# Weighing two steps' exponentials together in the last attention group, with seven tiles of exponentials in turn

## The chip, the cores and the metric

The kernel runs on one core of a Trainium2 chip. The metric is the device time of one execution in microseconds (us); the lower, the better. PE is TensorE, PEld its loading of weights, DVE is VectorE, ACT is ScalarE, POOL is GpSimd and SP is SyncE.

## The reference

One transformer layer over 4096 tokens of 256 features, all in float32: causal attention with 16 heads of 16 features, then a gated feed-forward network with 1024 hidden features, each between layer norms and with a residual.

```python
qkv = layernorm(x) @ w_attn + b_attn            # 16 heads of 16
logits = q @ k^T * 16 ** -0.5, causal
x = x + layernorm(softmax(logits) @ v @ w_proj + b_proj)
h = silu(xn @ w1^T * w1_s) * (xn @ w2^T * w2_s)  # xn = layernorm(x)
h = gelu(h @ h1^T * h1_s);  h = gelu(h @ h2^T * h2_s)
x = x + layernorm(h @ w3^T * w3_s)
```

## The kernel before

The tokens are cut into 8 blocks of 512 (QB), and a block into four tiles of 128 (P). The 16 heads are four groups of four. The attention's work is a list `items` of 32 pairs (j, g), block of queries and group of heads, in the order of j and then g. For an item the loop runs over `kt`, the tiles of 128 keys up to the diagonal: 4 (j + 1) steps, 32 in the last block. One step makes the scores of 128 keys by 512 queries for four heads, their exponentials, and the product of these with the values.

- **Scores** (`ScoreUnit`). A unit is one pair `pr` of the group's two pairs of heads. `products` (L664) issues four matmuls: keys by queries for either head, and a second product that subtracts each query's maximum (`mrow`, `ones`). They lie in half the array's rows each, in tiles of 64*128, and two run side by side. A unit's result fills two PSUM banks: either one tile of two banks of the pool `ps_s` (two such tiles), or, if the unit is `alone`, two single banks of the pool `ps_m` (three banks). Where no maxima are taken in the step, every third unit is alone.
- **Exponentials** (`finish`, L679). ACT writes them to a tile `e` of 128 by 2 by 512, from the pool `ep` with five buffers: one instruction of 1024 elements for a unit in `ps_s`, two of 512 for a unit alone. In the four steps on the diagonal, POOL then zeroes what lies above it (L684).
- **Weighing** (`Values.step`, L714). Four heads' exponentials are the moving operand, the values the stationary one, in tiles of 128*32, into one PSUM bank `av` of the pool `ps_av`, which has one buffer. Over an item's steps the products add up in this bank. The trace has eight matmul records for a step's weighing, two passes of four. After an item's last step ACT copies the bank to `av_sb` (L723) and SP stores it (L725). `Values` is a queue: `add` puts a step's tiles in with the time from which they may be weighed, `LAG` = 2 after it, and `step` weighs the foremost if it is due. `now` advances by two a step. So the weighing of step kt - 1 stands behind the scores of step kt.
- **Maxima** (`MaxUnit`, L581, L594, L598). The maxima of an item to come are found beside the scores of an item before it: products of TensorE into `ps_m`, reduced by DVE. `due` pairs of such units go with each step. When the last item begins, all maxima are done, `pairs` is empty, and its steps hold scores, exponentials and weighings alone.
- **Background work** (`bg`) goes on between the steps: norms and projections of other blocks. In block 7 it is finished before the last group.

Every engine executes its instructions in the order in which the program issues them (`manual_schedule`); the waits between engines and for free buffers follow from the tiles. The tags "o" and "T" of the pool `wk1` (one buffer each, 128 by 2 by 512) serve the projection (`Room.features`) and the features of a block that is prepared (`xT`).

After the last item the queue of `Values` is emptied, and `feed_forward` begins with products `za` (L1007).

Of the kernel before, what the change touches and what calls it, by code (L numbers as in the profile page):

```python
# [10 lines left out]
F32 = mybir.dt.float32  # L11
# [6 lines left out]
P = 128  # L18
QB = 512
# [48 lines left out]
def sandwich_kernel(  # L68
# [119 lines left out]
    def weight_pieces(key, tags):  # L188

        return {  # L190
            (c, o): piece(tag, f"{key}_{c}_{o}", F32R) for (c, o), tag in tags.items()
        }
# [7 lines left out]
    def load_pieces(src, tiles):  # L200
        for (c, o), t in tiles.items():
            nc.sync.dma_start(
                out=t.bitcast(F32), in_=src[c * P : (c + 1) * P, o * QB : (o + 1) * QB]
            )
# [133 lines left out]
    with ExitStack() as actx:  # L338
# [3 lines left out]
        wk1 = actx.enter_context(tc.tile_pool(name="wk1", bufs=1))  # L342
        qp = actx.enter_context(tc.tile_pool(name="qp", bufs=3))
        ep = actx.enter_context(tc.tile_pool(name="ep", bufs=5))
# [4 lines left out]
        def bank(name):  # L349
            return ps_m.tile([P, 512], F32, tag="m", name=name)  # L350
# [114 lines left out]
        def queries(j, g):  # L465

            qT[j, g] = [
                load_rows(f"q{pr}", f"q{pr}_{j}_{g}", "q", j, 4 * g + 2 * pr) for pr in range(2)
            ]
# [14 lines left out]
        def ask(n, kt):  # L484

            while asked[0] < len(chunks) and chunks[asked[0]][0] <= n + 2:

                if asked[0] >= RING and chunks[asked[0] - RING] >= (n, (kt - 1) // NT):
                    return
                if n >= 2 * G and kt % 2:  # L490
                    return
                keys(*chunks[asked[0]])
                if n >= 2 * G:
                    return
# [74 lines left out]
        class MaxUnit:  # L569
            def __init__(self, j, g, t, c, pr, n, mx, neg, mcol):  # L570
                self.at = j, g, t, c, pr
                self.n, self.mx, self.neg, self.mcol = n, mx, neg, mcol
                self.ps = {h: bank(f"pm_{j}_{g}_{t}_{c}_{h}") for h in (2 * pr, 2 * pr + 1)}
                self.diagonal = c == j
# [14 lines left out]
            def finish(self):  # L589
                j, g, t, c, pr = self.at  # L590
                n = self.n
                for h, ps in self.ps.items():
                    if not self.diagonal:
                        nc.vector.tensor_reduce(  # L594
                            self.mx[:, h, c : c + 1], ps[:, 0:n], AX.X, ALU.max
                        )
                        continue
                    nc.vector.tensor_tensor_reduce(  # L598
                        out=ps[:, 0:n],
                        in0=ps[:, 0:n],  # L600
                        in1=mask[:, QB - n : QB],
                        scale=1.0,
                        scalar=-3.0e38,
                        op0=ALU.add,
                        op1=ALU.max,
                        accum_out=self.mx[:, h, c : c + 1],
                    )
                if not (self.diagonal and pr == 0):
                    return False
                neg, mcol = self.neg, self.mcol  # L610
                nc.vector.tensor_reduce(
                    neg[:, t, :], self.mx[:, :, 0 : j + 1], AX.X, ALU.max, negate=True
                )
                if t < NT - 1:
                    return False
                high = stat.tile([P, NT, 4], F32R, tag="high", name=f"high_{j}_{g}")
                nc.vector.tensor_copy(high, neg)

                col = mcol.rearrange("p t (i pr e) -> p t pr i e", i=2, pr=2)
                by_pair = [a.rearrange("p t (pr i) -> p t pr i", pr=2) for a in (neg, high)]  # L620
                nc.vector.tensor_copy(col[:, :, :, :, 0], by_pair[1])
                nc.vector.tensor_tensor(col[:, :, :, :, 1], *by_pair, ALU.subtract)
                return True

            def to_rows(self):
# [12 lines left out]
                nc.vector.tensor_copy(mrow, ps)  # L638
                mT[j, g] = mrow

        class ScoreUnit:


            def __init__(self, j, g, kt, pr, alone=False):
                self.at = j, g, kt, pr
                c, tt = divmod(kt, NT)
                self.k = kT[G * j + g, c, pr][:, tt * P : (tt + 1) * P]
                self.diagonal = c == j
                self.q0 = tt * P if self.diagonal else 0
                name = f"s_{j}_{g}_{kt}_{pr}"  # L650

                if alone:
                    self.ps = [bank(f"{name}_{i}") for i in range(2)]
                else:
                    both = ps_s.tile([P, 2, QB], F32, tag="s", name=name)
                    self.ps = [both[:, i, :] for i in range(2)]
                self.sources = [p[:, None, :] for p in self.ps] if alone else [both]
# [14 lines left out]
            def finish(self):  # L672
                j, g, kt, pr = self.at
                q0 = self.q0
                e = ep.tile([P, 2, QB], F32, tag="e", name=f"e_{j}_{g}_{kt}_{pr}")
                at = 0
                for ps in self.sources:
                    n = ps.shape[1]
                    nc.scalar.activation(e[:, at : at + n, q0:], ps[:, :, q0:], AF.Exp)  # L679
                    at += n  # L680
                if self.diagonal:

                    at = e[:, :, q0 : q0 + P]
                    nc.gpsimd.affine_select(  # L684
                        out=at,
                        in_=at,
                        compare_op=ALU.is_ge,
                        fill=0.0,
                        base=0,
                        pattern=[[0, 2], [1, P]],  # L690
                        channel_multiplier=-1,
                    )
                return e
# [101 lines left out]
        items = [(j, g) for j in range(NB) for g in range(G)]  # L795
# [28 lines left out]
        values = Values()  # L824
# [27 lines left out]
        for n, (j, g) in enumerate(items):  # L852
            if n + 2 < len(items):
                queries(*items[n + 2])
            if g == G - 1 and j + 2 < NB:
                bg.finish(("prep", j + 2))

            if (j, g) == (NB - 2, 0):
                for key in ("w1", "w2"):
                    W[key] = weight_pieces(key, TAGS[key])  # L860
                    load_pieces(rounded[key], W[key])
            if (j, g) == (NB - 1, G - 2):
                for _ in halving:
                    pass
                bg.add(("norm", 0), norm_block(0, room, first_features), NORM)
            if (j, g) == (NB - 1, G - 1):
                W["h1"] = weight_pieces("h1", TAGS["h1"])
                load_pieces(rounded["h1"], W["h1"])
            item = j, g
            if g == G - 1:  # L870
                issued += len(ahead)
                ahead.clear()
            begun = issued
            goal = min(first[min(n + 2, len(items))] + LEAD, first[-1])
            for kt in range(count[n]):
                ask(n, kt)
                if (g, kt) == (0, 2) and j + 2 < NB:
                    bg.add(("prep", j + 2), prep(j + 2), PREP)
                due = begun + (goal - begun) * (kt + 1) // count[n] - issued
                pairs = [next(stream) for _ in range(due)]  # L880
                issued += due
                es = []
                if pairs:
                    issue(MaxUnit(*pairs[0][0]))
                es = [
                    issue(ScoreUnit(j, g, kt, pr, not pairs and next(alone)))
                    for pr in range(2)
                ]
                if pairs:
                    issue(MaxUnit(*pairs[0][1]))  # L890
                values.step(now + 1)
                for pair in pairs[1:]:
                    for args in pair:
                        issue(MaxUnit(*args))
                now += 2
                values.add(j, g, kt, max(kt - NT * j, 0) * P, es, now - 1)
                rows_of(now)
                bg.pace(count[n] - kt + count[n] * max(G - 2 - g, 0))
                if j > 0 and kt % 4 == 2 and kt < NT * j:
                    next(halving, None)  # L900
            rows_of(now + 2)
            if n == len(items) - 2:
                count_low()
# [230 lines left out]
```

## Time and profile before

| | us |
|---|---|
| median of three runs | 2488.5 (2483.43 to 2493.22) |
| the profiled execution, its own time | 2495.86 |
| its span in the profile | 2494.2 |
| busy: PE / DVE / ACT / POOL | 2395.7 / 1786.7 / 1309.1 / 561.6 |
| the last group, from its first score to the feed-forward's first product | 1728.49 to 1798.00 |

The profile is of one execution. Its page gives the busy time of each engine, the chain of work that ended last, and groups of instructions by line. The other views are answers about stretches of the same trace: instructions in order of time (start, length, engine, line, what is written from what; a wait stands in brackets with what ended it), and the busy time of each engine in a stretch, with the share of full speed that TensorE's clock was granted (PEclk). Records that follow each other on an engine and are of one kind are merged in the timeline ("x4"); a merged row has the start of its first record.

### The profile page before, as it was taken

Reading aid. Unit: us, or ns where it says so; the run is one execution under the profiler, and the core shown is the slowest. Engines: PE = TensorE matmul, PEld = TensorE weight load, DVE = VectorE, ACT = ScalarE, POOL = GpSimd, SP = SyncE. Lnnn points to the kernel's source line nnn. Section 1 sums busy time; section 2 is a strip of 40 time slices with the busy share of each in tenths; the row PEclk is TensorE's granted clock in tenths of the full one; section 3 lists DMA queues with packets and bytes.
Section 4 is the critical chain, followed back from the end, with each engine's and each line's share of the span. In section 5 each row is a group of like instructions: output and inputs, shape, how many; then the busy total and the mean of one; then the engine's idle time right before and its main releaser. Section 6 shows DMA issues by size and latency. Waiting matters only on the chain.

```text
span 2494.2 us, 40139 instructions
## 1 busy us (share of the span) xinstructions
PE 2395.7 (96%) x15237; PEld 1434.2 (58%) x15237; DVE 1786.7 (72%) x3838; ACT 1309.1 (52%) x1710; POOL 561.6 (23%) x898
## 2 busy tenths in 40 slices
PE   4899999999999999999999999999999999999998
PEld 2545545545554555455555555544488787887887
DVE  1667988888897989799999888986145535554553
ACT  1336666665675667666667667766822222222221
POOL 2325333423343233322422222000001200000000
PEclk8779999999999999999999999999999999999999
DMA  4444434323333322424222231111111100000000
GB/s 145 150 141 141 151 115 152 120 82 130 107 126 117 116 72 96 151 94 133 84 74 72 88 109 60 51 56 56 47 54 35 34 1 18 17 17 1 17 9 10
DMA packets 134825, 202.73 MB, mean 81 GB/s; under 512 B 14912, under 2 KB 59584, under 8 KB 134624
## 3 DMA queue, kind: packets, MB, share of 16 engines
q1 hardware_dynamic: 132672, 198.75, 24.3%
q8 instruction: 122, 2.00, 0.3%
q10 hardware_dynamic: 1776, 1.18, 0.2%
q14 instruction: 79, 0.65, 0.1%
q0 software_dynamic: 176, 0.15, 0.1%
HBM read 137.91 MB, written 62.13 MB: 80 GB/s over the span
## 4 chain that ended last, share of the span: by engine, by line
PE 82%; DVE 11%; issue 2%; DMA 2%; ACT 1%; POOL 1%; SPq 0%; ACTq 0%; POOLq 0%; DVEq 0%
PE av L714 20%; PE s L664 18%; PE z L1007 18%; PE pm L581 16%; DVE mx L594 3%; DVE pm L598 2%; PE pyf L1076 2%; DVE fa L1048 2%; PE pk L426 1%; PE py L249 1%; PE pv L543 1%; PE pq L426 1%; PE pmt L630 1%; PE za L1007 1%; PE zb L1007 1%
## 5 line engine op out<-in xcount | busy, mean ns | idle before, releaser
L679 ACT ACTIVATE e<-s 128x1024 f32<-128x1024 f32 (+3 forms) x1175 | 1039.1, 936 | 471.1 <-PE s L664 462.3
L594 DVE TENSOR_REDUCE mx<-pm 128x1 f32<-128x512 f32 x1792 | 1111.5, 682 | 153.0 <-PE pm L581 135.4
L581 PE MATMUL pm<-k,q 64*128 64x512 f32 (+3 forms) x2304 | 626.9, 456 | 33.0 <-DVE mx L594 18.6
L581 PEld LDWEIGHTS pm<-k,q 64*128 64x128 f32 x2304 | 325.1, 188 | 533.3 <-DVE mx L594 368.9
L714 PE MATMUL av<-e,v 128*32 128x512 f32 (+3 forms) x4608 | 582.5, 577 | 0.2 <-POOL e L684 0.2
L664 PE MATMUL s<-q,k 64*128 64x512 f32 (+3 forms) x2304 | 472.7, 391 | 4.4 <-ACT xT L533 1.2
L664 PE MATMUL s<-mrow,ones 64*128 64x512 f32 (+3 forms) x2304 | 458.9, 381 | 0.0
L598 DVE CUSTOM_DVE_ANT_0 pm<-pm,mask 128x384 f32<-128x384 f32 (+3 forms) x512 | 240.2, 517 | 78.6 <-PE pm L581 75.7
L1063 ACT ACTIVATE fb<-z,sh 128x512 f32<-128x512 f32 x128 | 88.1, 688 | 388.4 <-PE z L1007 367.2
L664 PEld LDWEIGHTS s<-q,k 64*128 64x128 f32 x2304 | 236.5, 189 | 71.7 <-issue 18.8
L664 PEld LDWEIGHTS s<-mrow,ones 64*128 64x128 f32 x2304 | 241.3, 189 | 38.3 <-DVE mrow L638 0.7
L684 POOL TENSOR_SCALAR_AFFINE_SELECT e<-e 128x256 f32<-128x256 f32 x256 | 102.3, 407 | 620.1 <-ACT e L679 618.0
L1007 PE MATMUL z<-hb_0h,h 128*128 128x512 f32 x512 | 200.8, 392 | 0.0
L1007 PE MATMUL z<-hb_0l,h 128*128 128x512 f32 x512 | 200.0, 391 | 0.0
L714 PEld LDWEIGHTS av<-e,v 128*32 128x32 f32 x4608 | 91.7, 108 | 143.6 <-issue 130.5
L173 POOL TENSOR_TENSOR rstd<-ve,neghalf 128x4 f32<-128x4 f32 (+1 forms) x22 | 20.7, 943 | 662.9 <-DVE ve L171 637.4
L977 DVE CAST hb_1h<-fb 128x512 fp32r<-128x512 f32 x64 | 27.8, 435 | 144.5 <-ACT fb L1063 144.5
L977 DVE CAST hb_0h<-fb 128x512 fp32r<-128x512 f32 x64 | 27.3, 427 | 138.7 <-ACT fb L1063 138.7
L1007 PEld LDWEIGHTS z<-hb_0h,h 128*128 128x128 f32 x512 | 96.8, 189 | 20.0
L1046 ACT ACTIVATE sl<-za,s 128x512 f32<-128x512 f32 x64 | 44.0, 689 | 122.2 <-PE za L1007 64.2
L1007 PEld LDWEIGHTS z<-hb_0l,h 128*128 128x128 f32 x512 | 96.7, 189 | 19.9
L1048 DVE SCALAR_TENSOR_TENSOR fa<-zb,s,sl 128x512 f32<-128x512 f32 x64 | 47.6, 745 | 72.2 <-ACT sl L1046 72.2
(247 smaller groups left out, 2437.8 us busy)
## 6 DMA issues: line engine op xcount, KB each, us to landing
k<-k SPq DMA_DIRECT2D x288, 256.0 KB
q<-q SPq DMA_DIRECT2D x64, 256.0 KB
x<-in_x_dram SPq DMA_DIRECT2D x16, 512.0 KB
k<-hik SPq DMA_DIRECT2D x32, 256.0 KB
k<-lok SPq DMA_DIRECT2D x32, 256.0 KB
q<-hiq SPq DMA_DIRECT2D x32, 256.0 KB
q<-loq SPq DMA_DIRECT2D x32, 256.0 KB
avd<-av_sb SPq DMA_DIRECT2D x32, 256.0 KB
```

Source lines behind the costliest of these rows:

```text
L426: nc.tensor.matmul(ps, lhsT=wqk[d][:, i * D + c * P : i * D + (c + 1) * P], rhs=xTs[j][:, d, :], start=(d == 0), stop=(d == DC - 1),)
L581: nc.tensor.matmul(ps[:, 0:n], lhsT=qT[j, g][pr][r, t * P : (t + 1) * P], rhs=kT[G * j + g, c, pr][r, 0:n], start=True, stop=True,)
L594: nc.vector.tensor_reduce(self.mx[:, h, c : c + 1], ps[:, 0:n], AX.X, ALU.max)
L598: nc.vector.tensor_tensor_reduce(out=ps[:, 0:n], in0=ps[:, 0:n], in1=mask[:, QB - n : QB], scale=1.0, scalar=-3.0e38, op0=ALU.add, op1=ALU ...
L664: nc.tensor.matmul(self.ps[i][:, self.q0 :], lhsT=(self.k, ones[pr])[m][r, :], rhs=(qT[j, g][pr], mT[j, g])[m][r, self.q0 :], start=(m == ...
L679: nc.scalar.activation(e[:, at : at + n, q0:], ps[:, :, q0:], AF.Exp)
L684: nc.gpsimd.affine_select(out=at, in_=at, compare_op=ALU.is_ge, fill=0.0, base=0, pattern=[[0, 2], [1, P]], channel_multiplier=-1,)
L714: nc.tensor.matmul(self.av[h * HW : (h + 1) * HW, q0:], lhsT=vb[kt // NT][:, kt % NT, o : o + HW], rhs=es[h // 2][:, h % 2, q0:], start=(k ...
L977: nc.vector.tensor_copy(hi, full)
L1007: nc.tensor.matmul(ps, lhsT=w[c], rhs=single(part[:, c, :]), start=(c == 0 and i == 0), stop=(c == kc - 1 and i == parts - 1),)
L1048: nc.vector.scalar_tensor_tensor(h, zb, s2[:, oc : oc + 1], sl, ALU.mult, ALU.mult)
L1063: nc.scalar.activation(h, z, AF.Gelu, scale=sc[:, oc : oc + 1])
```

## The change

In the last item the weighing is not called at even steps, and is called twice at odd ones. So two steps' scores follow each other, and then the weighings of the two foremost steps in the queue. The first odd step weighs the last step of the item before it and step 0. At step 3 steps 1 and 2 are weighed, and so on; the last step's is weighed after the loop, as before. As more exponentials are alive at a time, their tiles in the last item go in turn through seven homes: five times the pool `ep`, then the tags "o" and "T" of `wk1`. All other items take `ep` as before.

```diff
+        homes = cycle(range(7))
+
+        def exponentials(name, last):
+
+            n = next(homes) if last else 0
+            if n < 5:
+                return ep.tile([P, 2, QB], F32, tag="e", name=name)
+            return wk1.tile([P, 2, QB], F32, tag="oT"[n - 5], name=name)
+
         class ScoreUnit:
...
                 self.at = j, g, kt, pr
+                self.last = (j, g) == items[-1]
...
-                e = ep.tile([P, 2, QB], F32, tag="e", name=f"e_{j}_{g}_{kt}_{pr}")
+                e = exponentials(f"e_{j}_{g}_{kt}_{pr}", self.last)
...
-                values.step(now + 1)
+
+                if n < len(items) - 1:
+                    values.step(now + 1)
+                elif kt % 2:
+                    values.step(now + 1)
+                    values.step(now + 1)
```

## The prediction

> **What bounds the kernel now.** I began with the page: which engine carries the chain that ended last, and by which lines. I then cut out the one stretch that the change touches, the attention's last group (block 7, group 3), and read its waits.
>
> ```profile
> PE 82%; DVE 11%; issue 2%; DMA 2%; ACT 1%; POOL 1%; SPq 0%; ACTq 0%; POOLq 0%; DVEq 0%
> PE av L714 20%; PE s L664 18%; PE z L1007 18%; PE pm L581 16%; DVE mx L594 3%; DVE pm L598 2%; PE pyf L1076 2%; DVE fa L1048 2%; PE pk L426 1%; PE py L249 1%; PE pv L543 1%; PE pq L426 1%; PE pmt L630 1%; PE za L1007 1%; PE zb L1007 1%
> ```
>
> TensorE carries the kernel, and the two lines whose order changes (scores L664, weighing L714) are the largest. But the shares are of all 32 groups, and only one changes. The busy time by stretch gives that group its size: the first row is the group from its first score to the feed-forward, the second its 26 full steps (kt 2 to 27).
>
> ```profile
> core 0: us, PE busy (x) PEld busy (x) DVE busy (x) ACT busy (x) POOL busy (x), PEclk, DMA share, GB/s
> 1728.49:1798.00 69.51, 68.65 (x522) 27.83 (x521) 0.42 (x2) 61.90 (x87) 3.75 (x9) 0.97 0.05 19
> 1733.86:1789.13 55.27, 55.27 (x421) 21.61 (x418) 0.00 (x0) 51.41 (x70) 0.00 (x0) 1.00 0.00 1
> ```
>
> Only 69.5 of 2494.2 us can move, and a step takes 55.27 / 26 = 2.126 us. TensorE never stands idle, yet ACT is busy for 93% of that time: two engines are close together. The timeline of one step shows where TensorE loses time.
>
> ```profile
> 1744.49 0.50 PE L664 MATMUL s<-q,k 64*128 64x512 f32 x2
> 1744.83 0.40 PE L664 MATMUL s<-mrow,ones 64*128 64x512 f32 x2
> 1745.07 0.39 PE L664 MATMUL s<-q,k 64*128 64x512 f32 x2
> ...
> 1745.32 6.20 ACT L679 ACTIVATE e<-s 128x512 f32<-128x512 f32 x8 [0.18 <-PE s L664]
> ```
>
> ```profile
> 1748.20 0.61 PE L714 MATMUL av<-e,v 128*32 128x512 f32 x4
> ...
> 1748.74 0.50 PE L664 MATMUL s<-q,k 64*128 64x512 f32 x2
> ...
> 1749.08 0.40 PE L664 MATMUL s<-mrow,ones 64*128 64x512 f32 x2
> ...
> 1749.31 0.40 PE L664 MATMUL s<-q,k 64*128 64x512 f32 x2
> ...
> 1749.54 0.40 PE L664 MATMUL s<-mrow,ones 64*128 64x512 f32 x2
> ...
> 1749.87 0.64 PE L714 MATMUL av<-e,v 128*32 128x512 f32 x4
> ```
>
> Read starts, not durations. Pairs of score products follow each other after 0.23 us. The first pair after a weighing needs 0.34 until the next (+0.10), a weighing starts 0.33 after the last pair (+0.10), and the second half of a weighing (from 1748.20) needs 0.54 until the scores, where its first half (0.99 in all, by the chain below) needs 0.45 (+0.09). So one round trip, scores to weighing and back, costs about 0.29 us.
>
> **What the Trainium skill says.** "TensorEngine Tiling (Array Packing)", Key Properties: changing the tiling mode drains the engine. Scores use 64*128 tiles and weighings 128*32, so each step changes twice; the extra gaps agree. "ScalarE: Activation LUTs", What ACT_TABLE_LOAD costs: an ACTIVATE takes 186 ns + 0.833 ns an element and overlaps its neighbour by about 93 ns. That makes 1039 ns for 1024 elements; the rows by shape in this stretch say 1025 (and 597 for 512). So ACT takes a 1024-wide tile every 0.93 us, 1.9 us a step. "TensorE: Matmul & The Clock Gate", Part 1: TensorE's clock is halved after a too idle window of 3.4 us. The trace agrees, as shown with the entry below.
>
> **The change, part by part.** Each group of two steps is now: four score units (a unit is the products of one pair of heads and fills two PSUM banks), then two weighings.
>
> *Removed:* one round trip in two steps, 0.29 us, at most 16 times: 4.6 us. No instruction is added or removed, and no DMA changes place beside others.
>
> *The exponentials' buffers.* Just before a weighing six tiles are alive, so seven suffice. Tags o and T in wk1 are last read by block 6's projection, done near 1508 us by its rows (L249). Their cost is nothing, whether under five or seven names.
>
> *A new wait.* Units alternate over ps_s (two buffers of two banks) and, every third unit (alone), over two of ps_m's three banks. Hence a unit reuses the banks of the unit three before it. Today the trace shows no wait of TensorE for that. In a burst of four, the fourth unit would start 0.34 + 5 x 0.23 = 1.50 us after the first. But the first unit's exponential starts 0.83 us after its products (1745.32 - 1744.49) and takes 1.03, and TensorE resumes 0.05 after ACT (the copy of av_sb ends at 1797.95, za starts at 1798.00): 1.91 us. So the fourth unit **waits 0.41 us**, and both weighings, and the next burst, are queued behind it. Where first and fourth units are both alone, ps_m's third bank is free and the first half of the exponential (597 ns) releases the next: no wait. With period three against bursts of four, that is one burst in three.
>
> A burst with the wait: 1.91 + 0.23 + 0.33 + weighings 3 x 0.45 + 0.54 = 4.36 us, against 4.25 for two steps today: +0.11. Without it: 0.34 + 6 x 0.23 + 0.33 + 1.89 = 3.94: -0.31. The spacing between two weighings is the one number that the trace lacks: at least 0.43 (two passes of 512 columns at the 0.21 us that a pair of scores streams, estimated from the Clock Gate page's 215.7 ns), at most 0.54; I take 0.45, as between the halves. Of the 13 bursts of full steps (kt 2 to 27), 9 wait and 4 don't: 9 x 0.11 - 4 x 0.31 = **-0.25 us**. Bounds: no wait at all -4.0, every burst waiting with 0.09 lost between weighings +2.6.
>
> *Entry, kt 0 and 1.* The previous group's last weighing and kt 0's are now adjacent, and share the one ps_av buffer.
>
> ```profile
> 1729.82 1.94 ACT L679 ACTIVATE e<-s 128x1024 f32<-128x1024 f32 x2 [6.60 <-PE s L664]
> ...
> 1731.64 0.59 ACT L723 COPY av_sb<-av 128x512 f32<-128x512 f32 x1
> ...
> 1732.87 1.07 PE L714 MATMUL av<-e,v 128*32 128x512 f32 x8
> ```
>
> Today the copy that frees ps_av runs beside kt 1's scores. After, ACT has all of kt 1's exponentials ahead of it: four units from 1729.82 at 0.92 to 0.95 end near 1733.7, the copy near 1734.3, and kt 0's weighing starts at 1734.4 where it now starts at 1732.87: **+1.5 us** (bounds 0.8, if ACT's queue is ordered more kindly, and 2.0). TensorE then idles some 1.4 us of 3.4, 40%. The busy time by window shows what that does to the clock (column before DMA share):
>
> ```profile
> 1992.00:1995.40 3.40, 2.15 (x7) 0.78 (x6) 3.02 (x6) 0.35 (x1) 0.00 (x0) 1.00 0.00 0
> 1995.40:1998.80 3.40, 3.40 (x9) 2.64 (x9) 1.12 (x2) 0.69 (x1) 0.00 (x0) 0.50 0.02 5
> 2162.60:2166.00 3.40, 2.31 (x9) 1.13 (x7) 3.26 (x7) 1.19 (x1) 0.00 (x0) 1.00 0.00 0
> 2166.00:2169.40 3.40, 3.18 (x13) 2.42 (x14) 1.71 (x3) 0.69 (x1) 0.00 (x0) 1.00 0.02 5
> ```
>
> 37% idle halved the next window, 32% did not. So I count one halved window; a score pair takes 0.43 there against 0.23 (1729.09 to 1729.51), a step of estimated 3.4 against 2.13 us, and 3.4 us of it lose **1.3 us** (bounds 0 and 2.6, two windows).
>
> *Tail, kt 28 to 31.* Kt 29's weighing moves behind the last scores and covers the exponentials and POOL's masks, for which TensorE now waits 0.17 and 0.21 us before the last weighing: **-0.3 us** (bounds -0.6 and 0).
>
> *Sum:* -0.25 + 1.5 + 1.3 - 0.3 = **+2.2 us**. The profiled execution took 2495.86 us (span 2494.2 and 1.7 around it), so 2498.1 in its terms; it lies 7.4 us over the median 2488.5, so I forecast **2490.7 us**, within 0.5% (12.4 us, about what a measurement of this kernel can tell from no change).
>
> **Rivals.**
> 1. *The wait for banks doesn't come, the drains go.* For it: ACT needs about 1.9 us a step and the new step would take 1.97. Against it: the latency from scores to free banks, 1.9 us, is longer than three units. It gives -4.0 in the full steps, with entry and tail -1.5 to -4.3: about 2485.5.
> 2. *The clock falls again and again (slower).* The same Clock Gate page tells (A second HAM failure mode) of kernels whose small idle gaps between PSUM buffers keep halving it. Place: the 0.41 us waits, 12% of a window. For it: a window with little idle time can fall too. Against it: today none of the 16 windows of the full steps is halved, and 32% idle did not do it. Each halved window costs 1.3 us; from 8 on, with entry and tail, the kernel is slower by over 12.4 us; all 16 give about 2512.
> 3. *Nothing changes,* because weighings don't pair: a step pops only what is due. At odd kt both entries are due by the queue's own times, so this would need an error in my reading: 2488.5.
>
> **How the numbers follow.** My account 0.60, rival 1 0.27, rival 3 0.03, rival 2 0.10, of which half beyond 0.5%. Faster by over 0.5% would need the stretch to lose 12.4 of 69.5 us, more than all drains: only an unrelated shift of the runs gives it, 0.05. So faster 0.05, same 0.90, slower 0.05. The range takes my account's bounds (-3.8 to +7.2), rival 1, and half the spread of the runs (5 us), not all at once: 2481 to 2498.
>
> **What would show it.** Full steps: bursts of about 4.36, 4.36 and 3.94 us in turn; TensorE waiting about 0.4 us before the fourth unit, released by ACT e L679, in two bursts of three; a second weighing 0.45 after the first. Entry: a wait of TensorE for ACT av_sb L723 above 1 us, and PEclk 0.5 after it. I am wrong if the full steps' 55.27 us fall below 52 or rise above 58, or if anything outside 1728 to 1798 us moves.

## The result and the profile after

The changed kernel takes 2495.72 us (median of 22 runs), the kernel before 2491.93 us beside it: a ratio of 1.0017 with a 95% interval of 1.0010 to 1.0024, or 2.5 to 6.0 us more. A second comparison in another session (e9) gave 1.0013 (1.0005 to 1.0022). The change is slightly slower, within the 0.5% that was forecast as no change. The forecast rise of 2.2 us lies just below the first interval and inside the second (1.2 to 5.5 us). The forecast of 2490.7 us for the time itself was 5.0 us too low; 3.4 of these are that the kernel before took 2491.93 us here, and 2488.5 in the runs that the forecast started from.

The profiled execution took 2498.98 us with a span of 2497.3 us. Its chain has the same lines as before (the attention's moved by ten, so L674 is the scores, L724 the weighing, L689 the exponential, L733 the copy to av_sb; the feed-forward's by fifteen, so L1022 is `za` and `z`), with one that was not among the first: ACT's exponential, at 1%.

```profile
PE 81%; DVE 11%; DMA 2%; issue 2%; ACT 2%; POOL 1%; SPq 0%; ACTq 0%; POOLq 0%; DVEq 0%
PE av L724 20%; PE s L674 18%; PE z L1022 18%; PE pm L581 16%; DVE mx L594 3%; DVE pm L598 2%; PE pyf L1091 2%; DVE fa L1063 2%; PE py L249 1%; PE pk L426 1%; PE pv L543 1%; PE pq L426 1%; ACT e L689 1%; PE pmt L630 1%; PE za L1022 1%
```

The busy time by stretch, for the last group and for its 26 full steps. The columns after the length are the busy us of PE, PEld, DVE, ACT and POOL, PEclk, the DMA share and GB/s:

```profile
1728.22:1799.46 71.24, 66.35 (x522) 30.84 (x521) 0.42 (x2) 60.29 (x87) 3.66 (x9) 0.97 0.05 20
1735.23:1791.02 55.79, 53.58 (x420) 24.07 (x416) 0.00 (x0) 49.87 (x69) 0.00 (x0) 1.00 0.01 4
```

TensorE's busy time in the full steps fell from 55.27 to 53.58 us, yet they take 55.79. Half of the changes of tiling went, and with them the time lost at these, but idle time took its place and 0.5 us more. The view of waits, for TensorE in the last group, says what it is idle for (us in total, times, longest):

```profile
PE s L674 <- ACT e L689: 2.6, 10, 0.3
PE av L724 <- ACT av_sb L733: 1.6, 1, 1.6
```

Neither wait was in the trace before. Nine of the ten waits for ACT e fall in the full steps, one in the tail. The chain shows the bursts. Those with a wait run through ACT, and the one between them (from 1739.73) doesn't:

```profile
1735.30 0.69 PE s L674 x4
...
1736.07 1.03 ACT e L689
...
1737.14 0.73 PE s L674 x4
1737.88 1.85 PE av L724 x16
1739.73 2.14 PE s L674 x16
1741.87 1.85 PE av L724 x16
1743.72 0.68 PE s L674 x4
...
1744.48 1.03 ACT e L689
```

In the timeline one sees both waits with the time that TensorE was idle in brackets:

```profile
1733.60 0.58 ACT L733 COPY av_sb<-av 128x512 f32<-128x512 f32 x1
...
1734.23 1.06 PE L724 MATMUL av<-e,v 128*32 128x512 f32 x8 [1.65 <-ACT av_sb L733]
1735.23 0.50 PE L674 MATMUL s<-q,k 64*128 64x512 f32 x2
...
1737.14 0.50 PE L674 MATMUL s<-q,k 64*128 64x512 f32 x2 [0.24 <-ACT e L689]
1737.48 0.40 PE L674 MATMUL s<-mrow,ones 64*128 64x512 f32 x2
1737.81 1.92 PE L724 MATMUL av<-e,v 128*32 128x512 f32 x16
1739.66 0.50 PE L674 MATMUL s<-q,k 64*128 64x512 f32 x2
...
1743.65 0.50 PE L674 MATMUL s<-q,k 64*128 64x512 f32 x2
```

The fourth unit starts 1.91 us after the first (1737.14 - 1735.23). Without the wait it would start at 1736.73, 0.23 us after the pair at 1736.50, so the loss is 0.41 us. The bracket has only 0.24 us, because the third unit's last pair counts as busy until 1736.90: for a queue of matmuls the loss is read from starts. A burst with the wait takes 4.43 us (1735.23 to 1739.66), one without 3.99 (1739.66 to 1743.65), and two steps before the change took 4.25.

| part of the last group, us | before | after | difference |
|---|---|---|---|
| entry, to the first score of step 2 | 5.37 | 7.01 | +1.64 |
| full steps 2 to 27 | 55.27 | 55.79 | +0.52 |
| tail, to the feed-forward's first product | 8.87 | 8.44 | -0.43 |
| sum | 69.51 | 71.24 | +1.73 |

The span grew by 3.1 us. The rest stands in the feed-forward, which took 697.8 us from its first product to the end, against 696.2: its first cast, `ha_0h` (DVE), started 1.92 us after its input was ready in this execution, and 0.1 in the kernel before. Experiments e4, e7, e8 and e11 are about that.

### The profile page after: what moved, and what is told of

Read it like the earlier page. It is cut to its first block, busy times and chain, and to the rows that moved or that the text cites. A ratio compares the mean times of both kernels' runs of the same rounds, so it can differ in the third digit from the quotient of the medians.

```text
span 2497.3 us, 40138 instructions
## 1 busy us (share of the span) xinstructions
PE 2392.1 (96%) x15237; PEld 1437.6 (58%) x15237; DVE 1786.4 (72%) x3838; ACT 1307.3 (52%) x1710; POOL 561.4 (22%) x898
## 4 chain that ended last, share of the span: by engine, by line
PE 81%; DVE 11%; DMA 2%; issue 2%; ACT 2%; POOL 1%; SPq 0%; ACTq 0%; POOLq 0%; DVEq 0%
PE av L724 20%; PE s L674 18%; PE z L1022 18%; PE pm L581 16%; DVE mx L594 3%; DVE pm L598 2%; PE pyf L1091 2%; DVE fa L1063 2%; PE py L249 1%; PE pk L426 1%; PE pv L543 1%; PE pq L426 1%; ACT e L689 1%; PE pmt L630 1%; PE za L1022 1%
## 5 line engine op out<-in xcount | busy, mean ns | idle before, releaser
L689 ACT ACTIVATE e<-s 128x1024 f32<-128x1024 f32 (+3 forms) x1175 | 1037.4, 937 | 470.1 <-PE s L674 465.1
L724 PE MATMUL av<-e,v 128*32 128x512 f32 (+3 forms) x4608 | 577.3, 575 | 1.6 <-ACT av_sb L733 1.6
L674 PE MATMUL s<-q,k 64*128 64x512 f32 (+3 forms) x2304 | 472.4, 391 | 7.2 <-ACT e L689 3.1
L674 PE MATMUL s<-mrow,ones 64*128 64x512 f32 (+3 forms) x2304 | 459.6, 381 | 0.0
L674 PEld LDWEIGHTS s<-q,k 64*128 64x128 f32 x2304 | 237.1, 189 | 66.3 <-ACT e L689 13.7
L674 PEld LDWEIGHTS s<-mrow,ones 64*128 64x128 f32 x2304 | 241.8, 188 | 38.4 <-DVE mrow L638 0.7
L1022 PE MATMUL z<-hb_0h,h 128*128 128x512 f32 x512 | 200.9, 392 | 0.0
L1022 PE MATMUL z<-hb_0l,h 128*128 128x512 f32 x512 | 200.1, 391 | 0.0
L724 PEld LDWEIGHTS av<-e,v 128*32 128x32 f32 x4608 | 93.7, 109 | 147.6 <-issue 129.4
L1022 PEld LDWEIGHTS z<-hb_0h,h 128*128 128x128 f32 x512 | 96.9, 189 | 20.0
L1022 PEld LDWEIGHTS z<-hb_0l,h 128*128 128x128 f32 x512 | 96.7, 189 | 19.9
```

The source lines that it names most:

```text
L674: nc.tensor.matmul(self.ps[i][:, self.q0 :], lhsT=(self.k, ones[pr])[m][r, :], rhs=(qT[j, g][pr], mT[j, g])[m][r, self.q0 :], start=(m == ...
L724: nc.tensor.matmul(self.av[h * HW : (h + 1) * HW, q0:], lhsT=vb[kt // NT][:, kt % NT, o : o + HW], rhs=es[h // 2][:, h % 2, q0:], start=(k ...
L1022: nc.tensor.matmul(ps, lhsT=w[c], rhs=single(part[:, c, :]), start=(c == 0 and i == 0), stop=(c == kc - 1 and i == parts - 1),)
```

## The experiments

Two were the changed kernel itself (e9, e10) and one the kernel before (e8), for further profiles. Ratios are to the kernel before, with 95% intervals; one profile each gives the stretches.

**e1_entry: step 0 weighed as before.**

```diff
+                elif kt == 0:
+                    values.step(now + 1)
                 elif kt % 2:
```

> The changed kernel, but step 0 of the last item calls the weighing once, as before the change, so that the previous group's last weighing no longer stands beside step 0's and ACT's copy of the av bank has step 1's scores to hide behind; pairs from step 3 on as in the changed kernel. Theory (the entry costs the changed kernel 1.6 us, TensorE waiting for the copy av_sb): no wait of TensorE for av_sb above 0.1 us in the last group, first score to feed-forward 69.6 us instead of 71.2, ratio to before 1.0010. Rival (the rise lies elsewhere, in the full steps or in the feed-forward): first score to feed-forward stays above 71, ratio 1.0017.

```profile
1728.21:1797.92 69.71, 66.46 (x521) 30.69 (x521) 0.42 (x2) 60.29 (x87) 3.67 (x9) 0.97 0.06 22
1733.66:1789.45 55.79, 53.57 (x420) 24.04 (x416) 0.00 (x0) 50.30 (x70) 0.00 (x0) 1.00 0.00 1
```

The last group takes 69.71 us, 1.5 less than in the changed kernel; the full steps are the same to 0.01 us. No wait for av_sb is left before the last group's end. So the 1.5 us are the cost of the two neighbouring weighings at the entry. The ratio is 1.0003 (0.9993 to 1.0012), below the 1.0010 that was expected; its interval is too wide to decide alone.

**e2_banks: single banks for the first and fourth unit of each burst.**

```diff
-                    issue(ScoreUnit(j, g, kt, pr, not pairs and next(alone)))
+                    issue(ScoreUnit(j, g, kt, pr, kt % 2 == pr if n == len(items) - 1 else not pairs and next(alone)))
```

> The changed kernel, but in the last item the units that use two single banks are chosen by their place in the burst of four: always the first and the fourth (in the changed kernel every third unit). Theory (two bursts of three lose 0.45 us because the fourth unit waits for the first one's exponential to free its banks): no such wait in any burst, all 13 bursts of full steps at about 4.0 us, 51.9 us for steps 2 to 27 instead of 55.8, first score to feed-forward 67.2 us, ratio to before 1.0001. Rival (ACT's rate or the weighing's own time holds the burst at 4.3 us): steps 2 to 27 stay above 54.5 us, ratio 1.0015 or more.

The first row below is the last group, the second 12 of its 13 bursts of full steps:

```profile
1720.29:1790.15 69.86, 67.33 (x522) 36.65 (x521) 0.42 (x2) 60.89 (x98) 3.62 (x9) 0.95 0.06 21
1732.46:1781.63 49.17, 49.17 (x389) 26.75 (x385) 0.00 (x0) 46.20 (x72) 0.00 (x0) 1.00 0.00 1
```

TensorE's idle time is gone, and a burst takes 49.17 / 12 = 4.10 us. The edit changes only which units use single banks, so the wait was for the banks. The burst is shorter than the 4.25 us of two steps before, but longer than the 4.0 expected (e3 shows why): thirteen of them make 53.3 us, between the expected 51.9 and the rival's 54.5. The group's 69.86 us hold the entry's wait and, after it, one burst at a halved clock (5.39 us, 1.29 over the others). Ratio 0.9993 (0.9983 to 1.0004): below the changed kernel's 1.0017 (1.0010 to 1.0024), not clear of the kernel before.

**e3_both: both edits.**

> The changed kernel with both edits: step 0 weighs as before, and the first and the fourth unit of each burst use single banks. Theory: the gains of the two add, first score to feed-forward 65.6 us (69.5 before the change), ratio to before 0.9985, or 0.9992 if the feed-forward's first cast again waits 1.9 us for the store of av_sb as in the changed kernel's profile. Rival (the 4.6 us of drains can't be had, since ACT becomes the bound as soon as TensorE stops waiting): above 68 us, ratio 0.9995 or more.

The first row is the last group, the second 11 bursts. Then three rows of the timeline around the start of one burst:

```profile
1722.21:1789.21 67.00, 66.28 (x522) 35.58 (x521) 0.42 (x2) 61.00 (x98) 3.62 (x9) 0.97 0.07 23
1735.55:1780.68 45.13, 45.13 (x356) 24.40 (x352) 0.00 (x0) 42.97 (x68) 0.00 (x0) 1.00 0.01 1
```

```profile
1747.89 0.64 PE L674 MATMUL s<-q,k 64*128 64x512 f32 x2
1748.23 0.53 PE L674 MATMUL s<-mrow,ones 64*128 64x512 f32 x2
...
1748.71 2.00 ACT L689 ACTIVATE e<-s 128x512 f32<-128x512 f32 x3 [0.24 <-PE s L674]
```

The group takes 67.0 us, 2.5 less than before the change and 4.2 less than the changed kernel: the gains of e1 and e2 add. About 0.3 of the 2.5 is luck with the clock, which was halved for a shorter part of the entry (5.09 us to step 2's first score, 5.37 before the change). The gain is 1.4 us short of the expected 65.6, since a burst takes 45.13 / 11 = 4.10 us. The merged pair at 1747.89 is 0.64 us long and not 0.50: the unit's two halves start 0.15 us apart (1747.89 and 1748.04). The second starts 0.05 us after the end (1747.99) of ACT's first exponential of the fourth unit before it, whose bank it takes by the order of the pool. So a small wait for banks is left. ACT is busy for 42.97 of 45.13 us, 95%, and idle only 0.24 us before a burst's first exponential. So the rival was half right: ACT still has idle time, but every burst now runs close behind it. Ratio 0.9998 (0.9987 to 1.0010), which decides between neither.

**e4_tiles: the seven tiles alone, nothing paired.**

```diff
-                if n < len(items) - 1:
-                    values.step(now + 1)
-                elif kt % 2:
-                    values.step(now + 1)
-                    values.step(now + 1)
+                values.step(now + 1)
```

> The kernel before with the seven tiles of exponentials in turn alone: every step weighs as before, nothing is paired. Theory (the tiles' places cost nothing): first score to feed-forward 69.5 us, the feed-forward's first cast waits at most 0.2 us for the store of av_sb, ratio to before 1.0000. Rival (the tiles in o and T change what the feed-forward's first tiles must wait for, which is the 1.8 us that the changed kernel lost after the last group): the first cast waits 1.5 us or more, ratio 1.0007.

The last group took 69.17 us and its full steps 55.27, as before the change; the ratio is 1.0005 (0.9996 to 1.0013). The cast waited 1.43 us, near what the rival had foretold (1.5 or more) and against the theory; but e8 shows 1.55 us in the kernel before itself, and e1 with the same tiles 0.32. So the wait needs no tiles in o and T, and they don't always bring it.

**e5_never: no unit on single banks in the last item.**

```diff
-                    issue(ScoreUnit(j, g, kt, pr, not pairs and next(alone)))
+                    issue(ScoreUnit(j, g, kt, pr, n < len(items) - 1 and not pairs and next(alone)))
```

> The changed kernel, but in its last item no unit uses single banks: all alternate over the two double buffers, so a unit reuses the banks of the unit two before it and the suspected wait comes twice a burst. Theory (the latency from a unit's scores to its free banks, 1.91 us, sets the burst): third unit 1.91 us and fourth 2.83 us after the first, bursts of 5.35 us throughout steps 2 to 27, first score to feed-forward about 85 us, TensorE's clock not halved there (idle 1.2 of 5.35 us, 23%), ratio to before 1.0074. Rival (such idle gaps make the clock halve again and again): PEclk 0.5 in four windows or more of the full steps, first score to feed-forward above 90 us, ratio above 1.009.

TensorE's waits over 11 bursts, the starts of the first, third and fourth unit of one burst, and the busy time of the 11:

```profile
PE s L674 <- ACT e L689: 9.9, 22, 0.7
```

```profile
1748.70 0.50 PE L674 MATMUL s<-q,k 64*128 64x512 f32 x2
...
1750.61 0.50 PE L674 MATMUL s<-q,k 64*128 64x512 f32 x2 [0.71 <-ACT e L689]
...
1751.53 0.50 PE L674 MATMUL s<-q,k 64*128 64x512 f32 x2 [0.18 <-ACT e L689]
```

```profile
1743.35:1802.12 58.77, 48.91 (x356) 18.53 (x352) 0.00 (x0) 42.38 (x44) 0.00 (x0) 1.00 0.00 1
```

The third unit starts 1.91 us and the fourth 2.83 us after the first, as expected. 58.77 / 11 = 5.34 us a burst against 5.35 expected, and the clock stayed at full speed (1.00) with TensorE idle for 17% of the time by the records. The group took 87.1 us, 2 more than expected, of which one halved window after the entry is a part. Ratio 1.0070 (1.0047 to 1.0092). So the latency from a unit's scores to its free banks sets the burst, and these gaps didn't halve the clock.

**e6_five: the changed kernel with five tiles.**

```diff
-            n = next(homes) if last else 0
+            n = 0
```

> The changed kernel with the five tiles of exponentials of before also in the last item, none in o and T. Theory (what is waited for is PSUM and ACT; the fourth unit's exponential would have to wait for the first weighing of its burst, which is done before ACT gets there): bursts of 4.43, 4.43 and 3.99 us as in the changed kernel, first score to feed-forward 71.2 us, ratio to before 1.0017. Rival (seven tiles are needed for six alive): ACT waits for the weighing in each burst, bursts above 4.8 us, ratio above 1.003.

```profile
1723.06:1794.83 71.77, 66.51 (x521) 30.79 (x520) 0.42 (x2) 61.19 (x87) 3.70 (x9) 0.97 0.05 19
1730.07:1785.86 55.79, 53.57 (x422) 24.05 (x418) 0.00 (x0) 50.58 (x69) 0.00 (x0) 1.00 0.01 4
```

The full steps take the same 55.79 us with five tiles as with seven, so five tiles don't lengthen a burst. What differs is the tail, 0.5 us longer, where the last exponential waits for POOL:

```profile
1792.82 0.38 ACT L689 ACTIVATE e<-s 128x256 f32<-128x256 f32 x1 [0.54 <-POOL e L694]
```

Ratio 1.0011 (0.9999 to 1.0024).

**e8_before and e4 beside it: the cast's wait.** The kernel before, unchanged.

> The kernel before, unchanged, for a second profile. Theory (the wait of the feed-forward's first cast for the store of av_sb differs from execution to execution and is no part of the change): a wait other than the 0.1 us of the first profile, anywhere up to 1.9 us. Rival (the change makes it): 0.1 us again. First score to feed-forward 69.2 to 69.5 us under both.

The first row is of the first profile of the kernel before, the second of e8, the third of the changed kernel:

```profile
1802.16 0.43 DVE L977 CAST ha_0h<-fa 128x512 fp32r<-128x512 f32 x1
```

```profile
1798.25 0.43 DVE L977 CAST ha_0h<-fa 128x512 fp32r<-128x512 f32 x1 [1.55 <-SPq L1130]
```

```profile
1805.42 0.43 DVE L992 CAST ha_0h<-fa 128x512 fp32r<-128x512 f32 x1 [1.92 <-DMA h<-r_h]
```

The kernel before has the wait too, in another execution: it doesn't take the change to bring it. The brackets name a queue event in one and a load in the other, the event that ended nearest; e7 and e11 are about the store of av_sb.

**e7_both_store and e11_before_store: another place for the last av_sb.** e7 is e3 with this edit, e11 the kernel before with it:

```diff
-                    av_sb = wk1.tile([P, QB], F32, tag="av_sb", name=f"av_sb_{j}_{g}")
+                    name = f"av_sb_{j}_{g}"
+                    av_sb = (
+                        piece("k15_1", name)
+                        if (j, g) == items[-1]
+                        else wk1.tile([P, QB], F32, tag="av_sb", name=name)
+                    )
```

> The kernel with step 0 weighed as before and single banks for first and fourth unit, and the last item's av_sb in the tile of the last weights of h2 (k15_1) instead of wk1's, so that the feed-forward's first cast has no store to wait for. Theory (the cast ha_0h waits for the landing of the last store of av_sb, by chance 0.1 to 1.9 us): the cast waits under 0.1 us, 696.1 us from the feed-forward's first product to the end, first score to feed-forward 67.0 us, ratio to before 0.9985. Rival (the cast waits for other transfers, or the loads of h2 now come late): the cast waits over 1 us again or the products of h2 wait, 697.5 us or more from the feed-forward's first product to the end.

> The kernel before with the last item's av_sb in the tile of the last weights of h2 alone. Theory (the cast's wait for the store is there in most executions, and goes): the cast waits under 0.1 us, about 696.1 us from the feed-forward's first product to the end, ratio to before 0.9995. Rival (the wait only moves, or the weights of h2 come late): 697.5 us or more to the end, ratio 1.0000 or more.

The cast in e7; in e11 it stands 0.84 us after `fa` in the same way:

```profile
1796.51 0.75 DVE L1070 SCALAR_TENSOR_TENSOR fa<-zb,s,sl 128x512 f32<-128x512 f32 x1 [70.92 <-ACT sl L1068]
1797.35 0.43 DVE L999 CAST ha_0h<-fa 128x512 fp32r<-128x512 f32 x1
```

No wait is left in either. Of the eleven profiles with av_sb in wk1 nine have a wait of 1.4 us or more, one 0.32 and one 0.1, so two without any speak for the store; its landing itself is not in the records. From the feed-forward's first product to the end it is 696.3 us in e7 and 696.8 in e11 (which has one more halved window, near 2160 us), against 697.8 in the changed kernel. But the kernel before had 696.2 us in its first profile and 699.3 in e8 (with one more halved window too), so this stretch alone doesn't measure the edit. Ratios: e7 0.9991 (0.9981 to 1.0001), e11 0.9989 (0.9977 to 1.0001). They have the lowest ratios here, and neither is clear of the kernel before. e7's last group took 68.2 us, although the clock was halved for 6.4 us of its entry, and e11's 70.3. The full steps are where profiles repeat best: 55.27 us in all four with the order of before (the first, e8, e4, e11), 55.8 in the changed kernel's order at full clock (the first, e10, e6, e1), 53.4 in e3 and 53.2 in e7. So the pairing does gain 2 us there once the banks fit; the times of the whole kernel are too scattered to show it.

**e9_after and e10_after: the changed kernel again.**

> The changed kernel, unchanged, for a second profile. The last group's own rise was 1.7 us in the first profile, the ratio says 2.5 to 6.0 us. Theory (TensorE's 1.65 us wait at the entry halves the clock in some executions, for 1.3 us a window, according to how the window falls): the same 1.65 us wait and bursts, and either a window of PEclk 0.5 after it and 72.5 us from the last group's first score to the feed-forward, or none and 71.2; ratio to before 1.0012 to 1.0022. Rival (the rest is outside the last group): 71.2 us and something else longer than in both profiles of the kernel before.

> The changed kernel, unchanged, for a third profile, with the same expectations as for the second: 71.2 us from the last group's first score to the feed-forward without a halved window after the entry, 72.5 with one.

Busy time of the last group and of windows of its entry, e9 first:

```profile
1718.55:1791.16 72.61, 67.84 (x521) 31.33 (x520) 0.42 (x2) 60.29 (x87) 3.67 (x9) 0.94 0.06 21
1720.90:1724.30 3.40, 2.02 (x16) 0.81 (x12) 0.00 (x0) 3.19 (x5) 0.00 (x0) 0.50 0.29 108
1724.30:1727.70 3.40, 3.14 (x14) 1.28 (x16) 0.00 (x0) 0.21 (x1) 0.00 (x0) 0.50 0.20 77
```

```profile
1721.45:1792.68 71.23, 66.34 (x521) 30.81 (x520) 0.42 (x2) 60.28 (x87) 3.65 (x9) 0.97 0.06 21
1725.90:1729.30 3.40, 1.84 (x16) 0.87 (x18) 0.00 (x0) 1.51 (x3) 0.00 (x0) 1.00 0.20 77
```

Both have the wait of 1.65 us. After it the clock is halved for one more window in e9, and the group takes 72.61 us; not in e10, and it takes 71.23. So the halved window is real, costs 1.4 us, and is there in one execution of the same kernel and not in another. In e9 most of the wait (1722.91 to 1724.56) lies in a window that is itself halved; in e10 nearly all of it (1725.81 to 1727.46) lies in one at full speed. That fits the expectation, but how the window falls is not all. The first profile of the changed kernel and e5 have windows with the wait at full speed and TensorE busy for 1.75 of 3.40 us. The next window is at full speed in the former (first two rows) and halved in e5:

```profile
1732.50:1735.90 3.40, 1.75 (x18) 0.74 (x16) 0.00 (x0) 1.50 (x2) 0.00 (x0) 0.99 0.20 77
1735.90:1739.30 3.40, 3.16 (x30) 1.20 (x26) 0.00 (x0) 3.23 (x5) 0.00 (x0) 1.00 0.00 0
1734.40:1737.80 3.40, 1.75 (x20) 0.61 (x20) 0.00 (x0) 1.80 (x3) 0.00 (x0) 1.00 0.14 55
1737.80:1741.20 3.40, 3.07 (x16) 1.67 (x12) 0.00 (x0) 2.21 (x3) 0.00 (x0) 0.50 0.06 22
```

## Why the prediction was right

The sign of the rise was right, and so were the two waits that make it, the fourth unit's for banks and the entry's for the copy of av_sb. The size is near: 2.2 us forecast, 1.73 measured in the last group of the profile, 2.5 to 6.0 for the whole kernel (1.2 to 5.5 in e9's comparison). That the sum is so near is in part luck. The full steps cost 0.77 us more than forecast, and the halved window of 1.3 us was absent in the profile; the two errors offset each other. Step by step:

- **New wait for banks.** Forecast: the fourth unit 1.91 us after the first, in two bursts of three. Measured: 1.91, in nine of thirteen. e2 took it away, and e5 made it come twice in each burst.
- **The burst's length.** Forecast 4.36 and 3.94, measured 4.43 and 3.99. In the burst with the wait the fourth unit itself was mis-sized: after the wait its second pair comes 0.34 us after the first (1737.14 to 1737.48), as after a weighing, and I had set 0.23. In the burst without it the weighing starts 0.41 us after the last pair (1741.39 to 1741.80) and not 0.33; why is open. The price that the trace lacked, from one weighing to the next, was taken as 0.45; the chain's 1.85 us for two weighings, less 0.45 for the first half and 0.54 for the last, leaves 0.43 for each of the other two. So the full steps lost 0.52 us instead of gaining 0.25: this term had the wrong sign.
- **Entry.** Forecast +1.5, measured +1.64. The halved window after it, forecast at 1.3 us, was absent in the first profile and there in e9 (+1.4). Among six profiles with this entry, three have it (e2, e5, e9). Reading a threshold between 32% and 37% idle was wrong for the entry: windows with TensorE idle for 49% (the first profile, 1732.5 to 1735.9) and 46% (e10) were followed by full speed. The 37% window of the feed-forward is in all thirteen profiles (near 1992 us before the change), each time with a halved one after it. So the idle share alone doesn't tell, and the expected cost is nearer half of what I counted.
- **Tail.** Forecast -0.3, measured -0.43.
- **Buffers.** Free in the full steps, as forecast; five would have done there. In the tail five cost 0.5 us (e6), so the forecast of no cost held for seven alone.
- **Rivals.** The full saving of 4 us did not come, and e3 shows why: with the wait for banks gone a burst still takes 4.10 us. The recurring halving of the clock did not come even in e5. Its ground, that a window with little idle time can fall too, is in the trace before: TensorE was idle for 18% of 1411.70 to 1415.11 and 11% of 1452.65 to 1456.06, and both were followed by a halved window; why is open. That weighings pair is seen in the x16 of the timeline.
- **The sign of being wrong.** The full steps stayed within 52 to 58 us, but something outside 1728 to 1798 us did move: the feed-forward took 1.6 us more in the first profile. Since the kernel before took 3.1 us more there in e8 than in its own first profile, the change can't be held to be the cause.

**What stays open.** The last group gives 1.7 us, or 2.4 with a halved window in half of the executions. The cast's wait was 1.5 to 2.3 us in the six profiles with the changed kernel's entry, and 0.1 to 1.6 in the five with the entry of before whose av_sb is in wk1 (the kernel before twice, e1, e3, e4). If this is more than chance it adds about 0.9 us and makes up the rest; so few profiles don't settle it, and no experiment asks why the entry should delay a store 65 us later.

## What to carry to other kernels

Here, grouping work to save changes of TensorE's tiling paid only where the larger group found free PSUM banks: two steps took 4.25 us one by one, 4.43 grouped with the wait for banks, and 4.10 grouped with other banks (e2, e3). Compare the time in which the group fills them with the latency from a unit's start to its free bank, and let the units that need banks soonest have those that come free first. Look at the seams too: here two products for one accumulator became neighbours, and the wait for one copy at the seam cost more (1.64 us) than all bursts (0.52). And before a difference of 2 us between two profiles is explained, take a second profile of the kernel before.

## What was not expected of the hardware

- The Trainium skill's "TensorE: Matmul & The Clock Gate", A second HAM failure mode, tells of a kernel whose small idle gaps make the clock oscillate. In e5 TensorE was idle for 17% of 58.77 us, in two gaps per burst of 5.34 us, at PEclk 1.00: no oscillation in this kernel.
- A wait of 1.65 us, the same to 0.01 us in e9, e10 and the first profile, was followed by a halved window in one and not in two. TensorE's busy time in the window of the wait doesn't decide it: 1.75 of 3.40 us were followed by full speed in the first profile and by half in e5.
- The feed-forward's first cast, which by e7 and e11 waits for the last 256 KB store, was held by 0.1 to 2.3 us, in executions of one and the same kernel by 0.1 and 1.55.
